# Cross-attention block on one core: loads, exponentials and a store take other places in the engines' orders

## The chip, the core and the metric

The kernel runs on one core of one Trainium2 chip. A core has five engines, each with its own instruction queue: TensorE (PE: matmuls, and PEld: its weight loads), VectorE (DVE), ScalarE (ACT), GpSimd or Pool (POOL) and SyncE (SP), which here only issues transfers. ScalarE's queue issues transfers too. The engines wait for each other through semaphores; what stands in one queue runs strictly in the order written there. The metric is the device time of one execution in microseconds (us), smaller is better.

## The reference

One layer of cross-attention with a feed-forward part, in float32, over 128 batches of 128 tokens of width 256, 16 heads of 16, hidden width 1024. The mask is strict: position i sees only positions before i, and row 0 gets no attention at all.

```python
q = (x @ Wq + bq);  k = (c @ Wk + bk);  v = (c @ Wv + bv)   # each split into 16 heads of 16
scores = einsum('bhqd,bhkd->bhqk', q, k) / sqrt(16)
scores = where(j < i, scores, -1e30)
attn   = softmax(scores);  attn[:, :, 0, :] = 0
ctx    = einsum('bhqk,bhkd->bhqd', attn, v)
x1     = layer_norm(x + ctx @ Wo + bo, ln1_g, ln1_b)
out    = layer_norm(x1 + relu(x1 @ W1 + b1) @ W2 + b2, ln2_g, ln2_b)
```

## The kernel before

**Tiling.** The 128 batches go through in 64 pairs (`NP`); p numbers the pair. The scores of a pair are split by query: `hi = 1` is the upper 64 queries of both batches against all 128 keys (two tiles, t = 0 and 1, heads `ONE` and `TWO`), `hi = 0` the lower 64 queries, which the mask lets see only 64 keys. So a pair has three softmax tiles of 128 x 1024: (p, 1, ONE), (p, 1, TWO), (p, 0, ALL).

**The softmax** is a relay: TensorE `scores` -> VectorE `mask` (adds the mask, out of PSUM) and `maximum` (the maximum; Pool then subtracts it) -> ScalarE `exponential` -> VectorE `sums` (the sum and its reciprocal; Pool then multiplies). The attention matrix must then be transposed for `weigh`, the product with the values. There are two ways: `turn_on_pe` (TensorE transposes, ScalarE copies into `pT`), used for the first two pairs and the last; or, for all others, `turn` (VectorE transposes 32 x 32 blocks into `tb`) and `bring` (16 transfers that put the blocks into place in `pT`, eight issued on SP's queue, the others on ScalarE's).

**Behind it:** `weigh` -> `context` (ScalarE copies the result to `cxT`) -> `attention_out` (po) -> VectorE `attention_sum`, `attention_stats` -> `norm1` (x1) -> `turn_x1` or `turn_x1_on_pe` -> `hidden` (ph, ScalarE's ReLU into hT) -> `second` (py) -> `second_sum`, `stats`, `scale_and_shift`, `norm2` (ScalarE), `finish` (Pool, two products) and `store`, a transfer on ScalarE's queue.

**The order** is written out by hand (`manual_schedule`): the calls below stand in each engine's queue as they stand in the code. Pairs 0 and 1 have their own order (up to L778); `step(p)` (L793) is run for p = 2 to 62, and works on four pairs at once: the softmax of p, weigh and attention output of p - 1, hidden of p - 2, the second layer of p - 3. The branch `else` of `if p > 2` is for p = 2 alone. The last pair, behind the loop, again has its own order. In a step, the second half of `bring` goes out on ScalarE's queue between the ReLUs (`share`, L882); for p = 2 all eight go out behind the last ReLU:

```python
n = NS * NS - at if f == FC - 2 else 0 if f == 0 or p == 2 else NS // 2
bring(p, nc.scalar, range(at, at + n))
```

**Buffers and counters.** PSUM has four single banks (`ps_1`) and two double ones (`ps_2`, for scores). Each transfer counts up one of eight completion counters; the program takes them in turn over both queues, and before a transfer uses a counter again, its queue waits until the transfer that used it last has landed.

**The opening.** The first two pairs' tokens come in rows (`load_tokens`, `c_first`) and are transposed on TensorE (ptx, ptc); from pair 2 on they come in blocks (`load`) that VectorE transposes (`tokens`). The lines that the change touches: L129 (the first tokens of c, on SP's queue), L501 (`norm1`), L750 to L778 (pairs 0 and 1), L826 to L867 (the middle of a step) and L936 (the store in front of `second` and `weigh` of the last pair).

Of the kernel before, what the change touches and what calls it, by code (L numbers as in the profile page):

```python
# [19 lines left out]
def tile_cross_attention_block(  # L20
# [105 lines left out]
    load_tokens(0, slice(0, 2))  # L126
    wq = weight(Wq, "wq")
    c_first = const.tile([P, 4, D], F32, tag="c_first", name="c_first")
    nc.sync.dma_start(c_first[:, 0:2], c[0:2].rearrange("b p d -> p b d"))  # L129
    bq_c = column(bq, "bq_c")  # L130
    bk_c = column(bk, "bk_c")
    wk = weight(Wk, "wk")
# [109 lines left out]
    def tokens(p, which):  # L242
        st = states.setdefault(p, {})
        st[which + "T"] = proj.tile([P, KC, TP], F32, tag=which + "T", name=f"{which}T_{p}")
        nc.vector.transpose(
            st[which + "T"], blocks_of.pop((which, p)).rearrange("p k u f -> p k (u f)")
        )

    def add_bo(p):
        st = states[p]  # L250
        st["xb"] = proj.tile([P, 2, D], F32, tag="xb", name=f"xb_{p}")
        nc.gpsimd.tensor_tensor(
            st["xb"], tokens_of[p // 2][:, p % 2 * 2 : p % 2 * 2 + 2], bov_r[:, None, :].to_broadcast([P, 2, D]), ALU.add
        )
# [11 lines left out]
    def queries(p):  # L266
        st = states[p]
        st["qT"] = proj.tile([P, KC, TP], F32, tag="qT", name=f"qT_{p}")
        pq = project(wq, st["xT"], f"pq_{p}")
        for m in range(KC):  # L270
            nc.scalar.activation(  # L271
                st["qT"][:, m, :], pq[:, m * TP : (m + 1) * TP], AF.Identity,
                bias=bqs_c[:, m : m + 1], scale=QSCALE,
            )
# [41 lines left out]
    def scores(p, hi):  # L316

        st = states[p]
        n = P if hi else HP
        sps = [pair(f"pss{hi}_{p}_{t}") for t in range(2)]  # L320
        for m in range(KC):
            for s in range(2):
                first = s * P
                for r in range(NS):
                    strip = slice(32 * r, 32 * r + 32)
                    nc.tensor.matmul(  # L326
                        sps[r // 2][
                            s * HP : (s + 1) * HP, r % 2, m * 2 * n : (m + 1) * 2 * n
                        ].rearrange("p (e j) -> p e j", e=2),
                        st["qT"][strip, m, first + hi * HP : first + hi * HP + HP],  # L330
                        st["kT"][strip, m, :, first : first + n],
                        start=True, stop=True,
                    )
        st["sps", hi] = sps
        st["sm", hi] = soft.tile(
            [P, H, n], F32, tag=f"sm{hi}", name=f"sm{hi}_{p}", bufs=2
        )
        st["nmx", hi] = small.tile([P, H], F32, tag=f"nmx{hi}", name=f"nmx{hi}_{p}")
# [13 lines left out]
    def maximum(p, hi, part):  # L352
        st = states[p]
        n = P if hi else HP
        sm, nmx = st["sm", hi], st["nmx", hi]
        nc.vector.tensor_reduce(nmx[:, part], sm[:, part, :], AX.X, ALU.max, negate=True)  # L356
        nc.gpsimd.tensor_tensor(  # L357
            sm[:, part, :], sm[:, part, :],
            nmx[:, part, None].to_broadcast([P, part.stop - part.start, n]), ALU.add,
        )  # L360

    def exponential(p, hi, part):
        sm = states[p]["sm", hi]
        nc.scalar.activation(sm[:, part, :], sm[:, part, :], AF.Exp)  # L364
# [97 lines left out]
    def attention_out(p):  # L462
        st = states[p]
        po = st["po"] = bank(f"po_{p}")
        for s in range(2):
            for k in range(KC):
                nc.tensor.matmul(  # L467
                    po[:, s * D : (s + 1) * D], cxT[:, k, s, :], wo[:, k, :],
                    start=(k == 0), stop=(k == KC - 1),
                )  # L470
# [19 lines left out]
    def attention_sum(p):  # L490
        st = states[p]
        t1 = st["t1"] = ffn.tile([P, 2, D], F32, tag="t1", name=f"t1_{p}")
        nc.vector.tensor_tensor(
            t1, st.pop("po").rearrange("p (s d) -> p s d", s=2), st.pop("xb"), ALU.add
        )

    def attention_stats(p):
        stats(p, states[p]["t1"], 1)
        deviation(p, 1)

    def norm1(p):  # L501

        st = states[p]
        x1 = st["x1"] = ffn.tile([P, 2, D], F32, tag="x1", name=f"x1_{p}")
        t1, mv, sd = st.pop("t1"), st.pop(("mv", 1)), st.pop(("sd", 1))
        for s in range(2):
            nc.vector.tensor_scalar(  # L507
                x1[:, s], t1[:, s], mv[:, s, 0:1], sd[:, s], ALU.subtract, ALU.mult
            )
# [242 lines left out]
    mask(1, 1, 1)  # L752
    maximum(1, 1, TWO)
    add_bo(0)
    nc.gpsimd.tensor_tensor(be1b_r, be1_r, b2_r, ALU.add)
    turn_on_pe(0, 0, range(2))
    for which in "xc":
        tokens(2, which)
    weigh(0)
    context(0)  # L760
    scores(1, 0)
    exponential(1, 1, ONE)
    mask(1, 0, 0)
    mask(1, 0, 1)
    maximum(1, 0, ALL)
    attention_out(0)
    exponential(1, 1, TWO)
    attention_sum(0)
    attention_stats(0)
    queries(2)  # L770
    sums(1, 1, ONE)
    keys(2)
    norm1(0)
    exponential(1, 0, ALL)
    sums(1, 1, TWO)
    values(2)
    values_out(2)
    sums(1, 0, ALL)  # L778

    def load_ahead(p):  # L780
        if p % 2 == 0 and p + 4 < NP:
# [11 lines left out]
    def step(p):  # L793
        nonlocal waiting
        if p > 2:
            load_ahead(p)
        scores(p, 1)
        mask(p, 1, 0)
        maximum(p, 1, ONE)
        if p > 2:  # L800
            second(p - 3, 0)
            mask(p, 1, 1)
            maximum(p, 1, TWO)
            exponential(p, 1, ONE)
            second(p - 3, 1)
            if p + 2 < NP:
                tokens(p + 2, "c")
        else:
            turn_x1_on_pe(0)
            turn_on_pe(1, 1, range(2))  # L810
            fold_norm1()
            add_b1()
            hidden(0, range(FC // 2))
            mask(p, 1, 1)
            maximum(p, 1, TWO)
            exponential(p, 1, ONE)
            turn_on_pe(1, 1, range(2, 4))
            low_scores(p)
            hidden(0, range(FC // 2, 3 * FC // 4))
            turn_on_pe(1, 0, range(2))  # L820
            tokens(3, "x")
            add_bo(1)
        summed = []
        sums(p, 1, ONE)
        exponential(p, 1, TWO)
        if p > 2:  # L826
            second_sum(p - 3)
            summed = [p - 3]
        else:
            tokens(3, "c")  # L830
            load_ahead(2)
            load_tokens(2)
        sums(p, 1, TWO)


        weigh(p - 1)
        context(p - 1)
        if p > 2:
            scores(p, 0)
        if p == 3:  # L840
            scale_w1()
            nc.gpsimd.tensor_tensor(b1e_c, b1e_c, b1_c, ALU.add)
        queries(p + 1)
        if p > 2:
            mask(p, 0, 0)
            mask(p, 0, 1)
            maximum(p, 0, ALL)
        exponential(p, 0, ALL)
        turn(p, 1, 0)
        turn(p, 1, 1)  # L850
        for q in waiting:
            finish(q)
        if p == 2:
            add_bo(2)
        attention_out(p - 1)
        attention_sum(p - 1)
        sums(p, 0, ALL)
        attention_stats(p - 1)
        if p + 2 < NP:
            tokens(p + 2, "x")  # L860
            if p == 2:
                tokens(p + 2, "c")
        turn(p, 0, 0)
        bring(p, nc.sync, range(NS * NS // 2))
        keys(p + 1)
        norm1(p - 1)
        turn_x1(p - 1)  # L867
        values(p + 1)
        values_out(p + 1)
        for q in waiting:  # L870
            store(q)
        add_bo(p + 1)
        if p == 2:
            residual1(0)
        residual1(p - 1)
        for q in summed:
            stats(q, states[q]["t2"], 2)
        for q in summed:
            scale_and_shift(q)
        at = NS * NS // 2  # L880

        def share(f):  # L882
            nonlocal at
            n = NS * NS - at if f == FC - 2 else 0 if f == 0 or p == 2 else NS // 2
            bring(p, nc.scalar, range(at, at + n))
            at += n

        hidden(p - 2, range(0 if p > 2 else 3 * FC // 4, FC), share)
        for q in summed:
            norm2(q)  # L890
        waiting = summed
# [41 lines left out]
    turn_on_pe(p, 0, range(2))  # L933
    norm2(p - 3)
    finish(p - 3)
    store(p - 3)  # L936
    second(p - 2, 0)
    weigh(p)
    context(p)
    second(p - 2, 1, range(FC // 2))  # L940
    attention_out(p)
    second(p - 2, 1, range(FC // 2, FC))
    attention_sum(p)
# [77 lines left out]
```

## Time and profile before

| | us |
|---|---|
| three runs | 1595.31, 1599.59, 1599.91 |
| their median | 1599.59 |
| profiled execution | 1597.45 |
| its span | 1595.7 |
| TensorE busy | 1575.1 (99%) |
| VectorE busy | 1372.7 (86%) |
| Pool busy | 1282.0 (80%) |
| ScalarE busy | 756.4 (47%) |
| one step in the middle (py to py, 1502.91 to 1527.18) | 24.27 |

The page counts an engine as busy while it executes; waits, semaphores and the issue of transfers are not counted. A line of a timeline gives start, duration, engine, source line, operation, output <- inputs and how often; in square brackets stands the idle time before it and what ended that. A line of the waits gives who waited for whom, then the total in us, how often, and the longest. `ACTq` and `SPq` are the queues: there the duration of a transfer is the time to issue it, not to land it. "PEclk" is the clock that TensorE was granted, as a share of full speed.

### The profile page before, as it was taken

What the parts mean: (1) busy time and instruction counts of PE and PEld (TensorE: products, weight loads), DVE (VectorE), ACT (ScalarE), POOL (GpSimd) and SP (SyncE); (2) the same over time, 40 slices, a digit from 0 to 9 for tenths busy, and PEclk for the clock granted to TensorE, in tenths of its full rate; (3) what the DMA queues carried; (4) which work ended last, traced back from release to release, by engine and by line L of the source; (5) the groups of instructions that cost most, each with busy time, mean ns of one, the idle gap of its engine ahead of it and who ended that gap; (6) DMA issues with size and microseconds to landing.
All of it is one profiled execution on the core that took longest, in us unless ns stands there. A gap on an engine that the chain in (4) does not pass through costs nothing. (4 is left out here: it accounts for less than half of the span.)

```text
span 1595.7 us, 41275 instructions
## 1 busy us (share of the span) xinstructions
PE 1575.1 (99%) x16512; PEld 1328.6 (83%) x16512; DVE 1372.7 (86%) x1990; ACT 756.4 (47%) x1498; POOL 1282.0 (80%) x1104
## 2 busy tenths in 40 slices
PE   8899999999999999999999999999999999999998
PEld 6788888888888888888888888888888888888887
DVE  7889889888888988898988988889889989889862
ACT  4554454444444444444545444544444444454442
POOL 6878888887887888888888888878888888888882
PEclk9999999999999999999999999999999999999999
DMA  9455656556556556665565565565555665654430
GB/s 192 95 132 130 155 129 139 133 122 151 137 123 146 127 136 156 132 136 137 127 145 145 121 143 139 118 157 130 134 142 126 142 154 127 143 133 110 114 84 27
DMA packets 479935, 210.12 MB, mean 132 GB/s; under 512 B 348672, under 2 KB 448256, under 8 KB 479744
## 3 DMA queue, kind: packets, MB, share of 16 engines
q1 hardware_dynamic: 371376, 134.55, 38.2%
q10 hardware_dynamic: 108368, 72.92, 17.7%
q8 instruction: 131, 2.15, 0.6%
q14 instruction: 60, 0.49, 0.1%
HBM read 70.00 MB, written 33.03 MB: 65 GB/s over the span
## 5 line engine op out<-in xcount | busy, mean ns | idle before, releaser
L357 POOL TENSOR_TENSOR sm<-sm,nmx 128x1024 f32<-128x1024 f32 x192 | 364.3, 1897 | 123.3 <-DVE nmx L356 122.9
L640 PE MATMUL ph<-x1T,w 128*128 128x256 f32 x2048 | 453.4, 379 | 0.0
L658 PE MATMUL py<-w,hT 128*128 128x256 f32 x2016 | 453.0, 383 | 0.2 <-ACT hT L646 0.2
L658 PEld LDWEIGHTS py<-w,hT 128*128 128x128 f32 x2016 | 378.1, 190 | 73.2 <-issue 15.8
L378 POOL TENSOR_TENSOR sm<-sm,rs 128x1024 f32<-128x1024 f32 x192 | 364.3, 1898 | 92.7 <-DVE rs L377 89.9
L640 PEld LDWEIGHTS ph<-x1T,w 128*128 128x128 f32 x2048 | 388.8, 190 | 53.6 <-ACT x1T L625 0.5
L646 ACT ACTIVATE hT<-ph,b1e_c 128x256 f32<-128x256 f32 x504 | 208.7, 471 | 206.3 <-PE ph L640 105.1
L364 ACT ACTIVATE sm<-sm 128x1024 f32<-128x1024 f32 x192 | 200.8, 1053 | 207.0 <-POOL sm L357 197.6
L376 DVE TENSOR_REDUCE su<-sm 128x8 f32<-128x1024 f32 (+1 forms) x192 | 233.6, 1217 | 66.9 <-ACT sm L364 64.1
L345 DVE TENSOR_TENSOR sm<-pss,neg 128x1024 f32<-128x1024 f32 (+1 forms) x256 | 235.0, 939 | 54.0 <-PE pss L326 53.7
L391 DVE STREAM_TRANSPOSE tb<-sm 128x1024 f32<-128x1024 f32 x183 | 220.1, 1227 | 29.6 <-POOL sm L378 29.6
L356 DVE TENSOR_REDUCE nmx<-sm 128x8 f32<-128x1024 f32 (+1 forms) x192 | 234.2, 1220 | 6.6
L536 ACT ACTIVATE t<-t,nb,sd 128x256 f32<-128x256 f32 x124 | 67.7, 593 | 185.9 <-DMA pT<-tb 105.7
L260 PE MATMUL pq<-xT,wq 128*128 128x256 f32 x512 | 127.5, 392 | 0.0
L467 PE MATMUL po<-wo,cxT 128*128 128x256 f32 x512 | 122.5, 383 | 2.1 <-ACT cxT L460 2.1
L282 ACT ACTIVATE kT<-pk,bkh,half 128x256 f32<-128x256 f32 x252 | 120.6, 558 | 3.8 <-PE pk L260 3.8
L292 PE MATMUL pv<-wv,cT 128*128 128x256 f32 x512 | 121.0, 379 | 0.0
L260 PE MATMUL pk<-cT,wk 128*128 128x256 f32 x504 | 119.3, 379 | 1.0 <-issue 1.0
L326 PE MATMUL pss<-kT,qT 32*64 32x256 f32 (+1 forms) x4096 | 116.7, 335 | 0.4 <-ACT kT L707 0.2
L271 ACT ACTIVATE qT<-pq,bqs_c 128x256 f32<-128x256 f32 x128 | 53.6, 470 | 123.5 <-PE pq L260 123.5
L467 PEld LDWEIGHTS po<-wo,cxT 128*128 128x128 f32 x512 | 97.9, 191 | 16.2 <-ACT cxT L460 2.8
L515 POOL TENSOR_TENSOR x1b<-x,g_r 128x512 f32<-128x512 f32 x64 | 81.8, 1278 | 34.8 <-DVE x L507 34.8
(92 smaller groups left out, 1759.5 us busy)
## 6 DMA issues: line engine op xcount, KB each, us to landing
pT<-tb ACTq DMA_DIRECT2D x488, 96.0 KB, 2.7
pT<-tb SPq DMA_DIRECT2D x488, 96.0 KB, 2.9
out_dram<-t ACTq DMA_DIRECT2D x63, 256.0 KB, 2.5
xb<-in_x_dram SPq DMA_DIRECT2D x124, 128.0 KB, 4.4
cb<-in_ctx_dram SPq DMA_DIRECT2D x124, 128.0 KB, 4.3
x<-in_x_dram SPq DMA_DIRECT2D x31, 512.0 KB, 5.4
x1t<-tbx SPq DMA_DIRECT2D x248, 64.0 KB, 2.3
x1T<-x1t SPq DMA_DIRECT2D x62, 256.0 KB, 3.1
```

The source lines that it names most:

```text
L260: nc.tensor.matmul(ps[:, m * TP : (m + 1) * TP], w[:, k, m * P : (m + 1) * P], src[:, k, :], start=(k == 0), stop=(k == KC - 1),)
L345: nc.vector.tensor_tensor(st["sm", hi][:, part, :].rearrange("p (r n) j -> p r n j", r=2), st["sps", hi][t][:, :, : 4 * n].rearrange("p r ...
L356: nc.vector.tensor_reduce(nmx[:, part], sm[:, part, :], AX.X, ALU.max, negate=True)
L357: nc.gpsimd.tensor_tensor(sm[:, part, :], sm[:, part, :], nmx[:, part, None].to_broadcast([P, part.stop - part.start, n]), ALU.add,)
L364: nc.scalar.activation(sm[:, part, :], sm[:, part, :], AF.Exp)
L376: nc.vector.tensor_reduce(su, sm[:, part, :], AX.X, ALU.add)
L378: nc.gpsimd.tensor_tensor(sm[:, part, :], sm[:, part, :], rs[:, :, None].to_broadcast([P, part.stop - part.start, n]), ALU.mult,)
L391: nc.vector.transpose(st["tb"][:, :, at : at + 256].rearrange("p j (n a) -> p n j a", a=32), st["sm", hi].rearrange("p h j -> p (h j)")[:, ...
L467: nc.tensor.matmul(po[:, s * D : (s + 1) * D], cxT[:, k, s, :], wo[:, k, :], start=(k == 0), stop=(k == KC - 1),)
L640: nc.tensor.matmul(ph[:, i * TP : (i + 1) * TP].rearrange("p (s i a) -> p s i a", s=2, a=32), w1[:, k, (f + i) * P : (f + i + 1) * P], st[ ...
L646: nc.scalar.activation(st["hT"][:, f + i, :], ph[:, i * TP : (i + 1) * TP], AF.Relu, bias=(b1e_c if p else b1_c)[:, f + i : f + i + 1], sc ...
L658: nc.tensor.matmul(st["py"][:, s * D : (s + 1) * D], st["hT"][:, f, s * P : (s + 1) * P], w2[:, f, :], start=(f == 0), stop=(f == FC - 1),)
```

## The change

It has five parts.

- L129: the first tokens of c (pair 0) are loaded on ScalarE's queue instead of SP's. They become that queue's first transfer.
- Pairs 0 and 1: `scores(1, 0)` and `exponential(1, 1, ONE)` go in front of `weigh(0)` and `context(0)`; `tokens(2, "c")` goes behind the maximum of (1, 0); the exponentials of pair 1 go in front of the queries of pair 2; the sums of (1, 1) and (1, 0) move up on VectorE; the sum be1 + b2 moves behind them on Pool.
- `norm1(0)` uses a VectorE instruction with two tensors (t1, and the deviation read over and over along the row) instead of one with two scalars per partition. The other pairs keep the old one.
- Step p = 2: the exponential of (2, 0) goes in front of weigh(1) and context(1), its sums directly behind the sums of (2, 1), and `turn(2, 0, 0)` with SP's half of `bring` in front of `attention_stats(1)` and the tokens of pair 4; `add_bo(2)` moves behind the sums.
- The end: `store(p - 3)` goes behind weigh, context and the first half of the second layer's second batch.

All arithmetic stays; no matmul, no transfer and no exponential is added or removed.

```diff
-    nc.sync.dma_start(c_first[:, 0:2], c[0:2].rearrange("b p d -> p b d"))
+    nc.scalar.dma_start(c_first[:, 0:2], c[0:2].rearrange("b p d -> p b d"))
...
         for s in range(2):
+            if p == 0:
+                nc.vector.scalar_tensor_tensor(
+                    x1[:, s], t1[:, s], mv[:, s, 0:1], sd[:, s].to_broadcast([P, D]),
+                    ALU.subtract, ALU.mult,
+                )
+                continue
...
     add_bo(0)
-    nc.gpsimd.tensor_tensor(be1b_r, be1_r, b2_r, ALU.add)
     turn_on_pe(0, 0, range(2))
-    for which in "xc":
-        tokens(2, which)
+    tokens(2, "x")
+    scores(1, 0)
+    exponential(1, 1, ONE)
     weigh(0)
     context(0)
-    scores(1, 0)
-    exponential(1, 1, ONE)
     mask(1, 0, 0)
     mask(1, 0, 1)
     maximum(1, 0, ALL)
+    tokens(2, "c")
     attention_out(0)
     exponential(1, 1, TWO)
+    sums(1, 1, ONE)
     attention_sum(0)
     attention_stats(0)
+    exponential(1, 0, ALL)
     queries(2)
-    sums(1, 1, ONE)
+    sums(1, 1, TWO)
     keys(2)
     norm1(0)
-    exponential(1, 0, ALL)
-    sums(1, 1, TWO)
+    sums(1, 0, ALL)
+    nc.gpsimd.tensor_tensor(be1b_r, be1_r, b2_r, ALU.add)
     values(2)
     values_out(2)
-    sums(1, 0, ALL)
...
             load_tokens(2)
+            exponential(p, 0, ALL)
         sums(p, 1, TWO)
...
-        exponential(p, 0, ALL)
+        if p > 2:
+            exponential(p, 0, ALL)
+        else:
+            sums(p, 0, ALL)
+            add_bo(2)
         turn(p, 1, 0)
         turn(p, 1, 1)
         for q in waiting:
             finish(q)
-        if p == 2:
-            add_bo(2)
         attention_out(p - 1)
         attention_sum(p - 1)
-        sums(p, 0, ALL)
+        if p > 2:
+            sums(p, 0, ALL)
+        else:
+            turn(p, 0, 0)
+            bring(p, nc.sync, range(NS * NS // 2))
         attention_stats(p - 1)
...
-        turn(p, 0, 0)
-        bring(p, nc.sync, range(NS * NS // 2))
+        if p > 2:
+            turn(p, 0, 0)
+            bring(p, nc.sync, range(NS * NS // 2))
...
     finish(p - 3)
-    store(p - 3)
     second(p - 2, 0)
     weigh(p)
     context(p)
     second(p - 2, 1, range(FC // 2))
+    store(p - 3)
     attention_out(p)
```

## The prediction

> **What bounds the kernel now.** I read the page's busy table first, then TensorE's waits before and after 80 us, then timelines around the two places where TensorE stands still. The busy table and the waits after 80 us:
>
> ```profile
> PE 1575.1 (99%) x16512; PEld 1328.6 (83%) x16512; DVE 1372.7 (86%) x1990; ACT 756.4 (47%) x1498; POOL 1282.0 (80%) x1104
> ...
> PE po L467 <- ACT cxT L460: 2.1, 1, 2.1
> PE pc L438 <- DMA x1t<-tbx: 0.5, 1, 0.5
> PE py L658 <- ACT hT L646: 0.2, 1, 0.2
> ```
>
> TensorE is busy for 99%, and in more than 60 steps it waits almost nowhere: 2.8 us from 80 us to the end. No matmul is removed, so only TensorE's waits and slow stretches can give time back. The waits of the first 130 us:
>
> ```profile
> PE pc L438 <- DMA pT<-tb: 3.9, 1, 3.9
> PE ptp L421 <- POOL sm L378: 2.5, 3, 0.9
> PE ptc L226 <- DMA c_first<-in_ctx_dram: 1.6, 1, 1.6
> ...
> PE pc L438 <- ACT pT L423: 1.1, 4, 0.5
> PE pk L260 <- issue: 1.0, 1, 1.0
> PE ps_b L566 <- ACT vd L307: 0.3, 1, 0.3
> ```
>
> The two largest that the change touches are 3.9 us (weigh of pair 2) and, near the end, 2.1 us. Both leave a slow clock behind, as the windows show (last three columns: granted clock, DMA share, GB/s):
>
> ```profile
> 71.50:75.50 4.00, 0.09 (x2) 0.03 (x1) 3.33 (x4) 1.23 (x2) 3.79 (x3) 1.00 0.67 178
> 75.50:80.00 4.50, 4.50 (x132) 3.92 (x133) 3.29 (x7) 2.91 (x4) 3.80 (x3) 0.62 0.46 112
> 1553.00:1556.00 3.00, 1.78 (x8) 1.22 (x7) 0.00 (x0) 0.07 (x1) 2.52 (x2) 1.00 0.33 85
> 1556.00:1560.00 4.00, 3.15 (x9) 2.56 (x10) 0.00 (x0) 0.58 (x1) 0.00 (x0) 0.67 0.19 66
> ```
>
> The timelines tell what each wait is for. At weigh of pair 2, the two queues bring pT, and TensorE starts when SP's last piece is in:
>
> ```profile
> 63.47 0.84 ACT L646 ACTIVATE hT<-ph,b_c 128x256 f32<-128x256 f32 x2
> 65.61 5.13 ACTq L406 DMA_DIRECT2D pT<-tb  x8
> ...
> 65.74 7.85 SPq L406 DMA_DIRECT2D pT<-tb  x8
> ...
> 64.41 7.17 PE L658 MATMUL py<-w,hT 128*128 128x256 f32 x32
> 75.50 0.45 PE L438 MATMUL pc<-pT,vd 128*32 128x64 f32 x16 [3.91 <-DMA pT<-tb]
> ```
>
> At the end, ScalarE's queue stands at a store that waits for Pool, and the context copy behind it holds TensorE:
>
> ```profile
> 1551.98 1.09 ACT L536 ACTIVATE t<-t,nb,sd 128x256 f32<-128x256 f32 x2 [2.92 <-POOL nb L528]
> 1555.79 0.38 ACTq L551 DMA_DIRECT2D out_dram<-t  x1
> 1556.21 0.58 ACT L460 COPY cxT<-pc 128x508 f32<-128x508 f32 x1 [3.14 <-POOL t L543]
> ...
> 1556.85 3.32 PE L467 MATMUL po<-wo,cxT 128*128 128x256 f32 x8 [2.06 <-ACT cxT L460]
> ```
>
> **The change part by part.** The sum is made against the profiled execution, 1597.45 us (span 1595.7 and 1.75 around it); it lies 2.14 below the median of the three runs, 1599.59.
>
> *1. Last store behind the context copy and half of the second layer.* The copy then waits only for pc (ends 1552.86) and for the two norm2 activations (end 1553.07): it runs about 1553.1 to 1553.7. TensorE has py until 1554.6, so po no longer waits: minus 2.06. The slow clock goes too: po's eight matmuls took 3.10 from start to start against 1.73 usually, the next eight py 2.14 against 1.73, so 1.37 + 0.41 = 1.78. The store now waits for Pool (until 1555.77) with only hT behind it, which TensorE doesn't deliver before some 1560: covered. **3.8 us**, bounds 2.06 (clock stays slow) and 3.84.
>
> *2. Weigh of pair 2.* ScalarE exponentiates the low half directly behind exp TWO (53.97 to 55.0; Pool's maximum ended 53.9). The context copy moves from 54.65 to 55.0, ends 55.6, and po needs it at 56.36: covered by the queries of pair 3. VectorE then sums the low half at 55.8 instead of 60.64, Pool scales it 58.86 to 60.72 (add_bo(2) goes behind it, to 62.0, and ve needs its input at 63.1: covered), and the transpose into tb runs at 60.75 instead of 64.38, in front of statistics and the two token transposes. So tb is whole at 61.95, not 65.58. What is late next? Not VectorE but the queues. ScalarE's first piece stands behind hT in its queue; the wait before it was already reached at 63.5 (the queue's own record at that line), so it goes out at about 63.6, not 65.61: A, the start, moves 2.0. SP may start at 62.0, but the built program gives both queues eight completion counters in turn, and a piece waits until the last user of its counter has landed. In the trace SP's third piece went out at 69.78, after ScalarE's third (66.92) plus 2.86; its fifth at 71.07, ScalarE's fifth (68.21) plus 2.86. In the new order SP's third waits for ScalarE's second, its sixth for ScalarE's fifth, its eighth for ScalarE's sixth. With 0.65 between issues: third at A + 0.65 + 2.86 = 67.1, sixth at A + 2.6 + 2.86 = 69.1, eighth at A + 3.25 + 2.86, or two behind the sixth: 70.35. It lands 2.5 later (before: 73.00 to 75.50), at 72.85. TensorE is there at 71.58: a wait of 1.3 instead of 3.91, **minus 2.6**. Bounds: 1.9 (ScalarE's start only after hT ends, 64.3) and 3.9 (pieces land in 2.1, the shortest here, and are all in).
>
> *3. The clock behind that wait.* pc, pss and pq took 2.36 + 1.08 + 2.04 against 1.48 + 0.62 + 1.83 one step later: 1.55. A wait of 1.3 lies between rows that left the clock at 1.00 (1.05 at 36.85; 1.61 at 6.39, where the eight pq took the usual 1.89) and one that did not (2.06). I take full clock: **minus 1.55**, bounds 0 and 1.55.
>
> [...]
>
> *4. First tokens of c on ScalarE's queue.* c is issued at 0.78 instead of 1.79, but beside x (0.79). Three loads of 256 KB (x, wq, c) were in by 6.35, x by about 4.0 and one about every 1.2 after it. If x and c share the rate, both are in at about 5.15: the transposes of x start 1.1 later than now (4.06), those of c follow, VectorE copies xT at 5.9 to 6.6, and pq, also waiting for wq (6.35), starts at about 6.6 instead of 6.89. **Minus 0.3**, bounds minus 1.3 (x not delayed) and plus 0.9 (x as late as c is now). Two biases and a table load move 0.5 back on ScalarE, whose first work is at 8.82; the last small load waits there for wk to land (about 7.5): covered. On SP wk, wv and the second x move up by 0.5 to 1.9; TensorE needs that x at 12.2. The Pool waits of 2.5 follow from the scores and shift with them.
>
> *5. Pair 0 and 1.* scores(1, 0) moves before weigh(0), where it stood under the context copy (pss 30.89 to 31.6, copy 31.01 to 31.59): po still starts at 31.65, so nothing. exp(1, 1, ONE) goes in front of the copy: Pool is ready at 29.42, exp ends 30.5, pc ends 30.97: covered by 0.4. exp(1, 0) goes in front of qT (35.41 to about 35.85), which the scores need at 39.96. ScalarE then has no exponential at 40.15, so vd is copied about 0.9 earlier and ps_b's 0.30 wait goes: **minus 0.3**, bounds 0 and 0.3. The sums of (1,1) in front of attention_sum push t1 back by 0.6; x1 is due at 41.01 for ptn and is ready before 40.2. be1b_r moves behind Pool's last product, due at residual1 at 66: covered. The wait of 1.05 on issue at 36.85 I leave, bounds 0 and 1.05.
>
> norm1(0) becomes two-tensor instructions. The tensor_scalar pair took 2.27 at 37.27, while Pool ran from 37.49 to 39.39, and 0.73 at 1547.15 with Pool idle; the nearest rows of the new form took 0.47. Bounds 0.95 and 2.4 for the pair; either way ptn has x1.
>
> [...]
>
> *Sum:* 3.84 + 2.6 + 1.55 + 0.3 + 0.3 = 8.6. 1597.45 - 8.6 = 1588.85; on the median's scale 1590.99, say **1591.0**.
>
> **The rivals.** *R1, half of it:* pair 2's pieces still come 2 us late (A at 64.3) and the clock still drops: 3.84 + 1.9 + 0.6 = 6.3, 1593.3. For it: the 2.86 chain through ScalarE; against: the queue's record at 63.5. *R2, hidden anyway:* the lead of pair 2 is given back in step 3, because VectorE and Pool come only about 1 us earlier there, and the clock at the end stays slow: 2.06 + 0.6 + 1 = 3.7, 1595.9. For it: Pool ran from 62.27 to 75.3 with little pause. Against: in step 3 SP issued until 96.13, its pieces were in by about 98.6, and TensorE came at 101.31, so 2.7 of slack. *R3, slower:* the order of transfers on the two queues carries over, so that weigh waits in every step. It decides from 8.6 / 61 = 0.14 us a step beyond the slack; at 0.4 a step it would be 1591.0 + 24 = 1615. Against: the built program's counters from pair 3 to the last are the old ones. *R4, no effect of c's queue:* 0.3 less or, at its bound, 1.2 less: 1592.2, inside the range.
>
> **How the numbers follow.** Forecast with R4: 0.48; R1: 0.2; R2: 0.2; R3: 0.12. Within 0.3% (4.8 us) is about what this measurement can't tell from no change; the forecast and R1 are faster by more, R2 is not. Faster 0.68, same 0.20, slower 0.12. The range: all upper bounds (3.84 + 3.9 + 1.55 + 1.3 + 0.3 = 10.9, 1588.7) less the 2 to 3 by which runs differ, 1586; upward past R2, 1597, R3 left out.
>
> **What would show it.** po near the end waits for nothing and takes about 1.73 per eight; ScalarE's first piece of pair 2 at some 2 us earlier relative to py, SP's third some 2.9 behind ScalarE's second; pc's wait about 1.3 and the window behind it at 1.00; pq at about 6.6. I am wrong if that window still shows about 0.6, if ScalarE's pieces start only behind hT, if ptx starts past 5.5, or if pc waits appear past 80 us.

## The result and the profile after

The changed kernel took 1588.95 us (median of four runs, 1587.93 to 1589.91) against 1598.86 for the kernel before on the same chip: a ratio of 0.9942 with a 95% interval of 0.9925 to 0.9959, so some 9 us by the ratio (9.9 in the medians), 0.6% less. The prediction was 1591.0 (1586 to 1597). The profiled execution took 1587.93, its span 1586.2, against 1597.45 and 1595.7. Of all the runs below one is left out: a run of the kernel with the old norm1 took 2037.06, at a granted clock of 0.753.

Four marks on TensorE's queue cut the two spans in pieces: py of step 2 (64.41 before, 62.94 after), po of step 2 (80.98, 74.86), the last pair's first pc (1551.31, 1545.84) and the end (1595.7, 1586.2).

| stretch | before | after | gain |
|---|---|---|---|
| start to py of step 2 | 64.41 | 62.94 | 1.47 |
| py of step 2 to po of step 2 | 16.57 | 11.92 | 4.65 |
| po of step 2 to the last pair's first pc | 1470.33 | 1470.98 | -0.65 |
| that pc to the end | 44.39 | 40.36 | 4.03 |
| span | 1595.7 | 1586.2 | 9.5 |

So both large gains came from the places that the prediction named, and the 60 steps between gave nothing in these two executions. TensorE's waits in the first 130 us of the changed kernel (who waited for whom: total, how often, longest):

```profile
PE ptp L421 <- POOL sm L378: 2.5, 3, 0.9
...
PE pss L326 <- ACT kT L713: 1.3, 1, 1.3
PE pc L438 <- DMA x1t<-tbx: 0.8, 1, 0.8
...
PE po L467 <- ACT cxT L460: 0.7, 1, 0.7
...
PE ptn L226 <- DVE x L508: 0.2, 1, 0.2
```

The 3.9 at weigh of pair 2 is down to 0.8 (the profile puts it down to another transfer; SP's last piece of pT, issued at 68.25, is the one that should land then, 2.2 to 2.7 later). ptc no longer waits for c. New are 1.3 of the first scores for kT, 0.2 of ptn for x1, and 0.7 of pair 0's po for the context copy. This last one costs nothing: the scores that used to fill that time now stand in front of weigh, and po starts 0.31 earlier (31.65 to 31.34), as the second pair's ptx does. The timeline at weigh of pair 2 shows the two queues' pieces, and TensorE:

```profile
60.69 8.14 SPq L406 DMA_DIRECT2D pT<-tb  x8
...
62.00 0.47 ACT L652 ACTIVATE hT<-ph,b_c 128x256 f32<-128x256 f32 x1
62.06 0.60 ACTq L406 DMA_DIRECT2D pT<-tb  x1
...
62.70 4.53 ACTq L406 DMA_DIRECT2D pT<-tb  x7
...
62.94 7.17 PE L664 MATMUL py<-w,hT 128*128 128x256 f32 x32
70.92 0.44 PE L438 MATMUL pc<-pT,vd 128*32 128x64 f32 x16 [0.80 <-DMA x1t<-tbx]
```

ScalarE's first piece goes out beside hT, 0.88 in front of py; before, it was 1.20 behind it. At the end the context copy comes in front of the store, and po follows py without a gap (timeline of the changed kernel):

```profile
1547.32 2.00 PE L664 MATMUL py<-w,hT 128*128 128x256 f32 x8
1547.51 0.58 ACT L460 COPY cxT<-pc 128x508 f32<-128x508 f32 x1
...
1549.15 1.89 PE L467 MATMUL po<-wo,cxT 128*128 128x256 f32 x8
1550.34 0.38 ACTq L557 DMA_DIRECT2D out_dram<-t  x1
```

And the windows behind both places (last three columns: granted clock, DMA share, GB/s) stand at full clock, where before had 0.62 and 0.67:

```profile
72.00:74.00 2.00, 2.00 (x72) 1.63 (x61) 1.83 (x3) 1.21 (x3) 1.13 (x2) 1.00 0.27 76
...
1548.00:1552.00 4.00, 4.00 (x21) 3.52 (x20) 0.89 (x2) 0.10 (x1) 2.23 (x2) 1.00 0.35 112
```

In the opening the early c did not help as much as its transfer. TensorE starts pq at 5.85, 1.04 earlier than before, but the first scores at 10.86, 0.10 later. The chain on the way, from the timelines of ScalarE's queue, VectorE, ScalarE and TensorE, first two lines of the kernel before, then the changed kernel:

```profile
1.86 0.42 ACTq L118 DMA_DIRECT2D bv_c<-in_L_xattn_bv_dram  x1
...
10.76 0.69 PE L326 MATMUL pss<-kT,qT 32*64 32x256 f32 x16 [0.25 <-ACT kT L707]
```

```profile
4.63 0.39 ACTq L118 DMA_DIRECT2D bv_c<-in_L_xattn_bv_dram  x1
...
8.59 0.29 DVE L696 COPY bvw<-bv_c 128x256 f32<-128x256 f32 x1 [1.54 <-DMA bv_c<-in_L_xattn_bv_dram]
8.79 0.17 DVE L699 TENSOR_SCALAR bqs_c<-bq_c 128x2 f32<-128x2 f32 x1
...
9.06 0.84 ACT L271 ACTIVATE qT<-pq,bqs_c 128x256 f32<-128x256 f32 x2 [5.24 <-DMA g_c<-in_L_xattn_ln_g_dram]
...
10.86 1.12 PE L326 MATMUL pss<-kT,qT 32*64 32x256 f32 x32 [1.29 <-ACT kT L713]
```

bv_c went out at 4.63 instead of 1.86: by the built program it waits on its queue for a completion counter, and the transfer that had used this counter last is now the large one of c (issued at 0.78, landed some 3.8 later, so at about 4.6). VectorE's bvw stands there for bv_c, bqs_c stands behind bvw, qT needs bqs_c, kT stands behind qT on ScalarE, and the scores need kT.

### The profile page after: what moved, and what is told of

Read it like the earlier page. It is cut to its first block, busy times and chain, and to the rows that moved or that the text cites. A ratio compares the mean times of both kernels' runs of the same rounds, so it can differ in the third digit from the quotient of the medians.

```text
span 1586.2 us, 41271 instructions
## 1 busy us (share of the span) xinstructions
PE 1572.0 (99%) x16512; PEld 1329.7 (84%) x16512; DVE 1373.7 (87%) x1990; ACT 756.7 (48%) x1498; POOL 1282.1 (81%) x1104
## 4 chain that ended last, share of the span: by engine, by line
PE 95%; DMA 1%; DVE 1%; POOL 1%; issue 1%; SPq 0%; ACT 0%; ACTq 0%; POOLq 0%; DVEq 0%
PE ph L646 28%; PE py L664 27%; PE pq L260 7%; PE po L467 7%; PE pv L292 7%; PE pk L260 7%; PE pss L326 7%; PE pc L448 3%; PE pc L438 2%; DMA vd<-vz 0%; PE ptp L421 0%; POOL sm L378 0%; DMA x1t<-tbx 0%; DVE sm L345 0%; DMA c_first<-in_ctx_dram 0%
## 5 line engine op out<-in xcount | busy, mean ns | idle before, releaser
L542 ACT ACTIVATE t<-t,nb,sd 128x256 f32<-128x256 f32 x124 | 67.7, 593 | 187.0 <-DMA pT<-tb 120.9
L260 PEld LDWEIGHTS pq<-xT,wq 128*128 128x128 f32 x512 | 92.4, 190 | 20.9 <-issue 10.3
```

Source lines behind the costliest of these rows:

```text
L260: nc.tensor.matmul(ps[:, m * TP : (m + 1) * TP], w[:, k, m * P : (m + 1) * P], src[:, k, :], start=(k == 0), stop=(k == KC - 1),)
```

## The experiments

The theory: three costs of the kernel before are gone, the wait at pair 2, the wait at the end, and the stretches of half clock that TensorE's idle time left behind. The rivals: one part alone carries it (the clock of the whole run, or c's queue); or the gain is noise of the opening. The first four kernels make one part each (the fourth two together, the order of pairs 0 and 1 and norm1), from the kernel before; the kernel before took 1598.5 beside them (21 runs).

**The store alone.**

```diff
-    store(p - 3)
     second(p - 2, 0)
     weigh(p)
     context(p)
     second(p - 2, 1, range(FC // 2))
+    store(p - 3)
     attention_out(p)
```

> The kernel before, with only the last store behind the context copy. If the wait of 2.06 and the slow clock behind it both came from the store (1.37 and 0.41 on the next sixteen matmuls): 3.8 us less, po waits for nothing, the window behind it at clock 1.00. If the clock drops there for another reason: 2.06 less and the window still near 0.67. If pc's wait at 71.5 stays 3.9, the parts don't touch each other.

Measured: 1594.14 (1592.24 to 1597.27), ratio 0.9977 (0.9967 to 0.9986). From the last pair's first pc to the end 40.39, as in the changed kernel; po waits for nothing. This is the predicted step, and it works alone. Pair 2 in that execution waited as before, 3.92, and paid more for it; the windows behind it:

```profile
72.00:74.00 2.00, 0.18 (x8) 0.62 0.63 152
74.00:76.00 2.00, 2.00 (x84) 0.50 0.31 74
76.00:78.00 2.00, 2.00 (x57) 0.50 0.53 146
78.00:80.00 2.00, 2.00 (x7) 0.67 1.04 164
```

Half clock from about 72.5 to 79.3 here (in the first window 0.38 x 2 x 2 us is slow, in the last 0.33 x 2 x 2): 6.8, twice the 3.4 (75.96 to 79.4) of the profile before, after the same wait. So the price of a wait changes from one execution to the next.

**Step 2 alone.**

```diff
+            exponential(p, 0, ALL)     # p = 2: in front of weigh(1), context(1)
...
+            sums(p, 0, ALL)            # directly behind the sums of (2, 1)
+            add_bo(2)
...
+            turn(p, 0, 0)              # in front of attention_stats(1)
+            bring(p, nc.sync, range(NS * NS // 2))
```

> The kernel before, with only the changes in step p = 2. If ScalarE's pieces then start 2 us earlier and SP's follow them through the shared counters: the wait of 3.91 falls to 0.8 to 1.3 and the clock behind it stays at 1.00, 4.2 to 4.7 us less; the end keeps its wait of 2.06 and its slow clock. If the earlier exponential of pair 2 were not what counts but the lead from pairs 0 and 1: the wait stays above 2 and the clock falls, less than 2 us less.

Measured: 1591.86 (1590.8 to 1593.82), ratio 0.9956 (0.9941 to 0.9971), 6.6 less, more than the 4.2 to 4.7 expected. The wait fell from 3.91 to 1.60, at full clock (1.00 in the windows from 68 to 78), but not to the 0.8 to 1.3 expected: here SP's first piece waited 3.1 for the transfer of vd on ScalarE's queue and went out at 63.49, 0.87 behind py, where the whole change has it 2.25 in front (60.69). tb was whole at 60.2, so the other parts of the change count here through the counters. The end is the old one: 2.07 of waiting and half clock behind it. In the timeline and windows of that execution:

```profile
71.40 0.45 PE L438 MATMUL pc<-pT,vd 128*32 128x64 f32 x16 [1.60 <-DMA pT<-tb]
...
1551.58 3.14 PE L467 MATMUL po<-wo,cxT 128*128 128x256 f32 x8 [2.07 <-ACT cxT L460]
...
1552.00:1554.00 2.00, 2.00 (x7) 0.57 0.10 35
1554.00:1556.00 2.00, 2.00 (x7) 0.58 0.00 0
```

**c's queue alone.**

```diff
-    nc.sync.dma_start(c_first[:, 0:2], ...)
+    nc.scalar.dma_start(c_first[:, 0:2], ...)
```

> The kernel before, with only c's first tokens on ScalarE's queue. In the changed kernel pq started 1.04 earlier (6.89 to 5.85), the first scores 0.10 later, the transposes behind them 0.31 earlier. If that lead is lost because VectorE's bqs_c stands behind bvw, which waits for bv_c, and bv_c's transfer now waits for c's: pq 1.0 earlier, qT no earlier than 8.8, in all 0.3 us less or nothing that can be measured. If the lead was lost to the other parts of the change: scores 1 us earlier and 1 us less.

Measured: 1594.03 (1592.66 to 1594.97, six runs), ratio 0.9969 (0.9958 to 0.9981). Neither theory had a gain of 4.5. Its opening was not faster than the others (first scores 10.60; py of step 2 at 63.05, against 62.72 and 62.62 in the two runs above, with c on SP's queue). What it did not have is a slow clock, although both waits were there (lines of its timeline, then of its windows):

```profile
73.73 0.45 PE L438 MATMUL pc<-pT,vd 128*32 128x64 f32 x16 [3.50 <-DMA x1t<-tbx]
...
1555.10 1.99 PE L467 MATMUL po<-wo,cxT 128*128 128x256 f32 x8 [2.07 <-ACT cxT L460]
...
74.00:76.00 2.00, 2.00 (x125) 1.00 0.30 69
...
1556.00:1558.00 2.00, 2.00 (x11) 1.00 0.00 0
```

A wait of 3.50 kept the clock here, one of 2.07 lost it in the run above. So length alone does not decide.

**Pairs 0 and 1 alone** (the order and norm1).

```diff
+    tokens(2, "x"); scores(1, 0); exponential(1, 1, ONE)   # in front of weigh(0)
...
+    sums(1, 1, ONE)          # in front of attention_sum(0)
...
+    exponential(1, 0, ALL)   # in front of queries(2)
...
+    nc.vector.scalar_tensor_tensor(...)                     # norm1(0)
```

> The kernel before, with only the order of pairs 0 and 1 and the new norm1(0). If that order is what removed the wait of 1.05 on issue in pk and of 0.30 at ps_b: ptp at 41.5 starts 1.0 to 1.2 earlier and py at 64.41 about 1.2 earlier. If the wait on issue was removed by the opening's loads coming earlier: py only 0.1 to 0.3 earlier. In both, pc's wait for pT stays 3.9, since it counts from ScalarE's queue, and the whole moves by as much as py.

Measured: 1597.76 (1594.97 to 1600.63), ratio 0.9996 (0.9986 to 1.0006): nothing that can be told from no change. Its profiled execution shows another cost of the opening (TensorE's timeline):

```profile
6.74 1.12 PE L226 MATMUL ptc<-ident,c_first 128*128 128x128 f32 x4 [1.62 <-DMA c_first<-in_ctx_dram]
7.64 3.62 PE L260 MATMUL pq<-xT,wq 128*128 128x256 f32 x8
11.06 2.78 PE L707 MATMUL pk<-cT,wk 128*128 128x256 f32 x8
```

Here c landed at 6.74 and the matmuls behind the wait took 3.62 and 2.78 instead of 1.89; py of step 2 came at 66.57. The granted clock reads 1.00 in these first microseconds (the windows from 3 to 15), so only the durations show it.

The gains of the four singles are 4.4, 6.6, 4.5 and 0.7, sum 16, against 9.9 together: they are not terms of a sum. Which of the other waits is followed by a slow clock differs from one execution to the next, as the windows above show (behind the 2.07 at the end 0.57 in one, 1.00 in another); that this explains the surplus is argued, not shown.

**The opening's gap filled.** For the next four kernels the kernel before took 1599.53 (17 runs).

```diff
     for which, first in (("x", ...), ("c", ...)):
+        if which == "c":
+            for i in range(7):
+                nc.tensor.transpose(warm[:, i % 4 * P : (i % 4 + 1) * P], ident, ident)
```

> The kernel before, with seven transposes of the identity added on TensorE between ptx and ptc, in the time in which TensorE waits 1.6 for the first tokens of c. They are extra work that nothing reads; no transfer moves. The question is why c on ScalarE's queue alone gained 4.5 in its runs, although its scores came only 0.2 earlier. Theory A (by filling TensorE's idle time in the opening it keeps the clock from dropping there: in the run of pairs 0 and 1 alone, where ptc waited 1.62, the eight pq took 3.62 and py of step 2 came 3.6 later than with c on ScalarE's queue): filled, the opening never runs cold, the eight pq take about 1.9 in every run, and the median is 2 to 4 below the kernel before, 1594.5 to 1596.5. Theory B (the gain was that the later waits, 3.5 and 2.07, happened to fall on harmless places, or that the data are earlier): filling changes nothing, 1597.5 to 1599.5, within 0.1% of the kernel before.

Measured: 1595.48 (1593.73 to 1599.23, 12 runs), ratio 0.9983 (0.9972 to 0.9993). Useless work on TensorE, with no transfer moved, made the kernel before faster, by 4.1 in the medians and 2.7 by the ratio. The median is inside theory A's range. The way is not shown, though: pq took 1.89 behind the fill, but so it did in the profile of the kernel before. What this execution gained lies elsewhere: 0.8 up to py of step 2, where the kernel before had 1.05 of "issue", 0.9 at pair 2 (a wait of 3.00 instead of 3.91) and 1.7 at the end, where the wait of 2.07 left no slow clock this time (1.00 in the windows from 1553 to 1563); the steps between took 1.35 longer. That the fill prevents cold openings like the one above fits the runs and stays a conjecture.

**c back on SP's queue**, from the changed kernel.

```diff
-    nc.scalar.dma_start(c_first[:, 0:2], ...)
+    nc.sync.dma_start(c_first[:, 0:2], ...)
```

> The changed kernel, with the first tokens of c back on SP's queue as in the kernel before; all else as changed. Theory A (c's queue is worth what the scores show, 0.3, and otherwise only counts where the opening runs cold): ptc waits 1.6 again, pq at about 6.9; 1589.0 to 1589.5 where the opening keeps its clock, and 3 to 4 more where it does not, so a wider spread than that of the changed kernel (1587.9 to 1589.9) and a median of 1589.3 to 1592. Theory B (c's queue is worth the 4.5 that it gave alone): 1593 or more in every run. Rival C (it is worth nothing at all): 1588.7 to 1589.2 and the same spread.

Measured: 1590.35 (1588.34 to 1591.9, six runs), ratio 0.9948 (0.9935 to 0.9962). The lowest is 0.4 above the changed kernel's, the highest 2 above its highest: as theory A had it, and far from B. In the profiled execution the scores even started at 10.38, 0.48 earlier than with c on ScalarE's queue, because c landed at 5.71 this time. Six runs do not settle whether the median differs.

**bqs_c in front of bvw**, from the changed kernel.

```diff
-    nc.vector.tensor_copy(bvw, bv_c[...])
     nc.vector.tensor_scalar(bqs_c, bq_c, QSCALE, None, ALU.mult)
...
     nc.vector.tensor_scalar(kT ...)          # keys of pair 0
+    nc.vector.tensor_copy(bvw, bv_c[...])
```

> The changed kernel, with one more move on VectorE in the opening: the scaled bias of the queries (bqs_c) goes in front, and the spread bias of the values (bvw), which waited 1.54 for bv_c, goes behind the keys of pair 0. Theory A (in the changed kernel the early queries, 5.85 against 6.89, do not reach the scores because bqs_c stands behind bvw: qT started 9.06, the scores 10.86): qT starts by about 8.4, right behind pq, the scores at about 9.9, unless kT holds them (kT waits for bk_c and pk, so no earlier than 10.2); the last chain then ends 0.6 to 0.9 earlier, 1588.0 to 1588.4 against 1588.95. Rival B (something else holds the scores: kT on ScalarE, behind the biases and the table load): qT earlier, but pss still at 10.8 to 10.9, and the time the same within 0.3.

Measured: 1587.91 (1587.56 to 1588.73, four runs), ratio 0.9934 (0.992 to 0.9949). The scores started at 9.79, 1.07 earlier: the chain above is right. But at py of step 2 (62.62) only 0.32 was left. The windows between show why:

```profile
24.00:26.00 2.00, 1.24 (x7) 0.73 1.04 119
26.00:28.00 2.00, 2.00 (x11) 0.50 0.87 309
28.00:30.00 2.00, 2.00 (x95) 0.92 1.11 363
```

Half clock from about 24.9 to 28.3. Ahead of it TensorE had waited twice for Pool, 0.94 and 0.76, work that the changed kernel does as well, without a drop in its two profiles.

**The counters at pair 2**, from the changed kernel: the loads of step 2 behind SP's pieces.

```diff
-            load_ahead(2)
-            load_tokens(2)
...
             bring(p, nc.sync, range(NS * NS // 2))
+            load_ahead(2)
+            load_tokens(2)
```

> The changed kernel, with the loads of step 2 (load_ahead(2) and load_tokens(2)) moved on SP's queue from in front of its pieces of pT to behind them. So the eight completion counters fall differently on the pieces: SP's third no longer uses the counter of ScalarE's second. Theory A (what is left of the wait at weigh of pair 2, 0.80, is SP's pieces held by those counters: third 65.16 = 62.70 + 2.46, eighth 68.25): SP's eight go out 0.65 apart, the eighth at about 65.2 and landed at about 67.9; ScalarE's last, 66.62, lands at about 69.5, in front of the end of py at 70.1; pc's wait goes from 0.80 to 0 to 0.2, and the time from 1588.95 to about 1588.2. Rival B (not the counters, but the transfers' own rate or VectorE's tb): SP's third still at about 65.2, the wait still 0.8. A third way: the loads of pairs 4 and after come 4 us later, and a wait for x or c appears in step 3; then the time is that wait longer.

Measured: 1589.51 (1588.71 to 1589.77), ratio 0.9943 (0.9928 to 0.9958): no gain. It is half of theory A. SP's eight did go out without a stop, the last at 65.6 instead of 68.2; but ScalarE's last came at 67.7 instead of 66.6, and a piece took longer to land. From the view of line 406, first of the changed kernel:

```profile
L406 SPq DMA_DIRECT2D pT<-tb x8: 507/588/592, 60.7 to 68.2; - x8
L406 ACTq DMA_DIRECT2D pT<-tb x8: 601/608/647, 62.1 to 66.6; - x8
...
DMA to landing us min/median/max: 2.2/2.4/2.7
```

and of this kernel (issue in ns: least, median, most; then the first and last start):

```profile
L406 SPq DMA_DIRECT2D pT<-tb x8: 508/590/630, 60.8 to 65.6; - x8
L406 ACTq DMA_DIRECT2D pT<-tb x8: 514/606/836, 62.2 to 67.7; - x8
...
DMA to landing us min/median/max: 2.8/3.1/3.4
```

With both queues issuing together each piece took 0.7 longer, and TensorE waited 0.98. The counters set the order of issue; the end of the sixteen transfers did not come earlier. One more wait came up in step 3, 0.56 of ph for ScalarE's exponential.

**Both late waits filled**, from the kernel before. For the last four kernels the kernel before took 1598.37 (17 runs).

```diff
         pc = bank(f"pc_{p}")
+        if p == 2:
+            for i in range(15):
+                nc.tensor.transpose(pc[:, i % 4 * P : (i % 4 + 1) * P], ident, ident)
...
         po = st["po"] = bank(f"po_{p}")
+        if p == NP - 1:
+            for i in range(8):
+                nc.tensor.transpose(po[:, i % 4 * P : (i % 4 + 1) * P], ident, ident)
```

> The kernel before, with transposes of the identity added on TensorE where it waits: 15 in front of weigh of pair 2 (wait 3.91; seven of them took 1.56 in an earlier run, so 15 take about 3.3), 8 in front of the attention output of the last pair (wait 2.06; about 1.75). Nothing reads them, no transfer and no other engine's work moves, so the data come when they came; only TensorE isn't idle any more. Theory A (each of the two waits costs twice: the wait, and a stretch of half clock behind it, which follows from TensorE's idle time): the weigh of pair 2 and the last po start as late as before, but both windows behind them stand at 1.00, and the time is 1.55 + 1.78 = 3.3 lower than before, a median of 1595 to 1596.5. Theory B (the slow clock comes from elsewhere, such as the load of the transfers, and only stands beside the waits): the windows still show 0.5 to 0.7 and the time is that of before, 1598.5 to 1599.5.

Measured: 1595.21 (1593.02 to 1598.15, 12 runs), ratio 0.9983 (0.9974 to 0.9992): 3.2 less in the medians, 2.7 by the ratio, where theory A had 3.3. The transposes were shorter than expected (1.80 for 15), so 2.31 and 1.21 of waiting stayed, but the clock held:

```profile
76.00:78.00 2.00, 2.00 (x52) 1.00 0.24 68
...
1554.00:1556.00 2.00, 1.34 (x6) 1.00 0.37 131
1556.00:1558.00 2.00, 2.00 (x11) 1.00 0.00 0
```

Weigh starts 11.12 behind py, as before (11.09), but py to po of step 2 takes 15.07 instead of 16.57, and the last pair's first pc to the end 42.72 instead of 44.39: 1.50 and 1.67, where theory A had 1.55 and 1.78. No transfer and no other engine's work was moved, so this separates the two costs: with part of TensorE's idle time filled the clock stayed at 1.00 beside the same transfers, and the gain was that of the clock alone. It is one profile, and unfilled waits too sometimes keep the clock (c's queue alone, above); so the median of the twelve runs carries this more than the windows do.

**The old norm1 with bqs_c moved.**

```diff
-            if p == 0:
-                nc.vector.scalar_tensor_tensor(
-                    x1[:, s], t1[:, s], mv[:, s, 0:1], sd[:, s].to_broadcast([P, D]),
-                    ALU.subtract, ALU.mult,
-                )
-                continue
```

> The changed kernel with bqs_c moved up in the opening (as in the run before, 1587.91) and with the old norm1 for pair 0, one instruction with two scalars per partition. Theory A (the two-tensor form is slower beside Pool, 2.52 against 2.27 for the pair, and its x1 came 0.20 late for ptn): the pair takes about 2.3 again, ptn waits for nothing, and the time is 0 to 0.2 lower, 1587.7 to 1587.9. Rival B (the old form takes longer here because Pool's sum now runs beside it in another place): 2.5 or more, the same time.

Measured: 1589.58 (1589.0 to 1591.54, five runs), above the 1587.7 to 1587.9 expected. VectorE's pair of instructions (shortest, median, longest ns), first in the changed kernel, then here:

```profile
L508 DVE SCALAR_TENSOR_TENSOR x<-t,mv,sd x2: 484/1302/2120, 37.4 to 37.8; 128x256 f32<-128x256 f32 x2
```

```profile
L507 DVE TENSOR_SCALAR x<-t,mv,sd x2: 414/1202/1990, 37.1 to 37.5; 128x256 f32<-128x256 f32 x2
```

The pair took 2.52 in the new form and 2.32 in the old, and ptn's 0.20 is gone: the norm1 part of the change is a small loss, too small for the total. The median is within 0.2 of the changed kernel's beside it (1589.75, the last run below), so the gain of 1 from bqs_c does not show here, and again the clock dropped in the opening, 25.3 to 28.8.

**The three waits of ptp filled**, from the run above.

```diff
             pt = bank(f"ptp{hi}_{p}_{t}")
+            if p == 0 and t == ts[0]:
+                for i in range(3):
+                    nc.tensor.transpose(pt[:, i * P : (i + 1) * P], ident, ident)
```

> The kernel of the run before, with three transposes of the identity in front of each of the three waits of ptp (0.94, 0.76, 0.77) in pair 0. The profile with bqs_c moved up showed the scores 1.07 earlier, but half clock from about 24.9 to 28.3, behind two of these waits, and only 0.3 of the gain was left at py of step 2. [...] Rival B (the slow stretch came by chance in one execution, or the fill delays ptp itself): same as the run before within 0.3, or up to 0.6 slower.

Measured: 1588.77 (1587.98 to 1589.43, five runs), 0.8 below the run above and 1.0 below the changed kernel beside it. The fill left 0.46, 0.24 and 0.44 of waiting. The drop is gone, and py of step 2 starts at 62.40, the earliest of all profiles:

```profile
24.00:26.00 2.00, 1.76 (x15) 1.00 1.05 372
26.00:28.00 2.00, 1.56 (x15) 1.00 1.14 331
```

So the drop went with TensorE's idle time, in this one profile. With no drop the median was expected 0.3 to 0.9 below the run before, at 1586.9 to 1587.5; it came 0.8 below that run and 1.3 above the range, and the next run shows that the changed kernel, too, took 0.8 more on the chip of these last runs.

**The changed kernel once more.** Nothing is edited.

> The changed kernel itself once more, as the reference of the runs beside it: 1588.95 before, so 1588.3 to 1589.6, and between the lowest and the highest some 2 us, against 5 to 6 for the kernel before.

Measured: 1589.75 (1588.66 to 1590.16, six runs), ratio 0.995 (0.9937 to 0.9963), 0.15 above the range expected. Over all ten runs the changed kernel has 1587.93 to 1590.16. Its second profile has py of step 2 at 62.90 and 0.67 of waiting at pair 2, as the first; yet the last pair's first pc comes at 1548.06 instead of 1545.84, at full clock all the way. So some 2 us come and go in the 60 steps between, in waits too small to be told apart.

## Why the prediction was right

On the profiled execution's own scale it said 1588.85 and 1587.93 came. The two large steps came by the way that it gave; part of the rest is luck. By its steps:

- *Step 1, last store: 3.84, measured 4.03.* po waits for nothing and takes 1.73 until the next py; the store goes out at 1550.34 and nobody waits for it. The run with this edit alone gives the same 40.39 to the end.
- *Steps 2 and 3, pair 2: 2.6 + 1.55 = 4.15, measured 4.65* (3.11 of the wait, 1.54 of clock). ScalarE's first piece went out 2.1 earlier relative to py, as argued from the queue's record. The size that was off is the 2.86 from a piece to its counter's next user: SP's third left 2.46 behind ScalarE's second (62.70 to 65.16), its sixth 2.33 behind ScalarE's fifth (64.65 to 66.98), and the eighth at 68.25 landed with 0.80 of waiting, not 1.3.
- *Step 4, c's queue: 0.3, measured 0.31* at the second pair's tokens (ptx 12.22 to 11.91). But the way is not the one predicted, and that the number fits is luck, two errors that cancelled. x was held up by only 0.28 (its transposes at 4.34, not 5.1), so pq started at 5.85 and not at 6.6; and the scores got nothing of it. "The last small load waits there for wk to land: covered" failed: bv_c was late by the counter of c's own transfer, and that cost the scores 1.07, as the run with bqs_c moved shows. Comparing two executions also flatters the step: c on SP's queue landed from 5.64 to 6.74 over the profiles, and where it came early the scores started at 10.17 to 10.38, before the 10.60 to 10.86 with c on ScalarE's queue. What c's queue may have taken away is the late and cold opening of some executions; one profile shows such an opening (scores at 14.08), and that c's queue is what prevents it is not shown.
- *Step 5, pairs 0 and 1: 0.3, measured 0.3 less 0.2.* The wait of ps_b is gone; norm1's new form took 2.52, over its upper bound of 2.4 (the author's estimate; the old form had taken 2.27), and ptn waits 0.20 for x1. The "issue" wait of 1.05 that was left alone is gone too, but in the four runs of one part each as well: a chance of the profile before. Without it the opening gains 0.42 of its 1.47, less than the 0.6 predicted, and the whole span 8.45 instead of 9.5, where the sum was 8.6.

Of the rivals, R1 (pieces 2 later, clock still low) and R2 (lead given back in step 3, clock still low at the end) fell with the rows above: after 80 us TensorE waits 0.7 in all. R3 (waits in every step), which was to decide from 0.14 a step, fell likewise: 0.65 over 60 steps is 0.01. A small part of R2 or R3 may be true, though. From po of step 2 to the last pair's first pc, the profiles of the kernel before and of the six kernels made from it took 1469.99 to 1471.88 (mean 1470.9); the seven of the changed kernel and of those made from it took 1470.93 to 1473.37 (mean 1472.1). So some 1 us may be given back there; the two ranges overlap. R4 (c's queue without effect) stays open within 1 us: 1590.35 against 1588.95 and 1589.75, with overlapping runs.

What the prediction did not have is the variation. It took 2 to 3 us of run-to-run noise as given. Part of it in the kernel before is the clock. Each slow stretch whose ends the windows show lasted 3.4 (75.96 to 79.4 in the profile before, 24.9 to 28.3 with bqs_c moved), but for the one of 6.8. By the prediction's rows (1.61 holds, 2.06 slows) the length of one wait decided whether such a stretch follows; that was an estimate, and the profiles contradict it. The wait in front of the last po was 2.06 or 2.07 in five of them. Three show half clock behind it (the kernel before, step 2 alone, pairs 0 and 1 alone; 44.4 from the last pair's first pc to the end), two show 1.00 (c's queue alone, the opening's gap filled; 42.7). At pair 2 a wait of 3.50 held the clock (c's queue alone), and one of 3.00 did not (the opening's gap filled, 0.62 in the window from 74 to 76). The waits of 0.94 and 0.76 that stood in front of the drops at 24.9 and 25.3 stand in the changed kernel's profile too, at 1.00. What decides, and why all six runs with only c's queue changed came out low, is not shown.

The changed kernel is faster for the two waits themselves, some 5 us, and for their slow clock, some 3; and its spread is 2.2 in ten runs against 6.6 in the 59 of the kernel before (standard deviation 0.7 against 1.8).

## What to carry to other kernels

A wait of 2 us on TensorE, otherwise always busy, cost 2.3 where the clock held and 4.0 where it did not (42.70 and 44.39 against 40.36 from the last pair's first pc to the end), and no run showed what decides which; look at the granted clock in narrow windows behind every wait, and judge a change by its runs' spread as well as by its median. When a large transfer takes over another queue, follow the completion counters and the in-order engines behind each small load that it pushes back: here a load of a few bias values took back 1 us of an earlier start. And a term that is read from two executions is as uncertain as the landing of their first transfers.

## What the runs showed of the hardware

- Useless matmuls in a wait can make a kernel faster: 7 transposes in the opening's gap, 4.1 lower in the median; 23 in the two late waits, 3.2. On the changed kernel with bqs_c moved and the old norm1, 9 more gave 0.8, on five runs each, which is at the edge of what these can tell.
- A slow stretch lasted 3.4 where TensorE was busy all through it, but for 0.2 in one, and 6.8 where the wait reached 1.3 into it (the store alone: drop at about 72.5, wait until 73.81).
- Sixteen pieces of pT issued from two queues at once landed in 3.1 each (median, the counters at pair 2) instead of 2.4 in the changed kernel; issuing them earlier did not make the last one land earlier.
- The two-tensor form of norm1 was slow beside Pool like the one with scalars. In the changed kernel Pool ran from 37.65 to 39.69, and the second instruction, in that time, took 2.12 against 0.48 for the first; the form with scalars took 1.99 and 0.41 there (the old norm1 with bqs_c moved), and 0.73 for both at 1547.15 of the kernel before, with Pool idle.
